# A two-layer graph kernel: two buffers for the divided weighted sums, their parts served after every product, and four changed places in the order

## The chip, the cores and the metric

The kernel runs on one core of a Trainium2 chip, all in fp32. A core has the engines TensorE (PE in the profile; PEld is its load of weights), VectorE (DVE), ScalarE (ACT) and GpSimd (POOL), and SyncE (SP), which here issues most of the DMAs. Each engine issues its instructions in the order in which the program has them; they wait for one another by semaphores. The metric is the time of one execution in microseconds of device time, smaller is better, as the median of several runs.

## The reference, cut to what matters

128 graphs of 64 nodes with 768 features go through two layers. `x` is (128, 64, 768), `adj` (128, 64, 64).

```python
# layer 0
u = h @ h.T / sqrt(d);  delta = softmax(u) * adjacency
attn = delta / (sum(delta) + 1e-10)
ctx = upper(attn) @ (h @ W_left.T + b_left) + diag(attn) * (h @ W_self.T + b_self) \
    + lower(attn) @ (h @ W_right.T + b_right)
x = layernorm(x + relu(normalise(ctx) * gamma + beta))
# layer 1, 12 heads of 64
q, k, v = heads(x @ Wq + bq), heads(x @ Wk + bk), heads(x @ Wv + bv)
s = where(adj > 0, q @ k.T / 8 + beta * adj, -9e15)
x = layernorm(x + softmax(s) @ v)
```

The part that the change is about is the last line: the product of the exponentials with `v`, its division by the row sums, and its addition to `x`.

## The kernel before, in words

The 8192 tokens are worked on in 16 blocks (`NBLK`) of 512 tokens: 8 graphs, held as 4 tiles of 128 rows. The loop over `n` (from L1205) interleaves three blocks: while block n does layer 1, block m = n+1 does layer 0, and block p = n-1 is finished (scores and weighted sums of its second group of heads, normalisation, store). In one turn of the loop TensorE does the left and right products of layer 0 for m, its self product, then values, queries and keys of layer 1 for n.

**Products.** All big products are done by schemes with fewer multiplications than the plain product, which need sums of inputs (POOL) and sums of outputs (DVE, some on ACT). The self product goes by `by_tokens` (matmuls L520, evictions L551 and L727). Left and right go by `side_part` (L756) for m below `DEEP` = 3, and for the 13 blocks from m = 3 by `both_sides` and `nested`: 49 sub-products of 7 groups of 7. Their matmuls are L784, their weights (`wlr`) come by DMA (L775). Each sub-product accumulates in one of two kinds of PSUM banks, X or Y. X takes the sub-products 1, 6, 7 and 4 of a group one after the other, Y takes 2, then 5 and 3, and DVE (L574) or ACT (L572) reads a bank between two of them: a late eviction holds up the next product of that bank. POOL adds the parts of the outer scheme (L581 to L589) and the inputs of the next group (`second_level`, the four sums of `q`, L472 to L475). Values, queries and keys go by `products`, a scheme of fifteen (matmuls L459, evictions L945 for `v`, L972 and L975 for queries and keys).

**The second half of the attention.** `scores(n, m)` does the scores of a group of heads (L996), their maximum and subtraction on DVE (L1008, L1012), the exponentials on ACT (L1029, 16 instructions of 0.52 us) into `eT`, and two transposes of `eT` on DVE, `turn` (L1033), of 0.97 us each. The two head groups use `eT` one after the other. `weighted(n, m)` does the weighted sums: 96 small matmuls (L1059) into four PSUM banks `ps_y`. Then come four parts `added(h, r)`: DVE takes the reciprocal of the row sums (L1065) and multiplies into a tile `share` (L1067), and POOL adds `share` to the rows of `x` in two adds (L1070). `share` has one buffer, so the next part's L1067 waits for both adds of the part before. `finish` follows: squares on ACT (L1116), mean and variance (L1089, L1092), root (L1095), reciprocal and shift (L1098, L1099), normalisation (L1103), store by POOL's queue (L1107).

**What sets the order.** There is no scheduler: instructions stand on each engine in the order in which the Python code issues them. Small work is not issued at once but put on one of three queues, `first`, `urgent` and `lazy`, and after each product (in `nested`: sub-product) `step` takes at most some items off them (`of_queues`, from L156). An item may have a kind ("act", "root", "tiny", "free", "gap"...); the four parts `added` have none and stand in `first`. In `nested` the steps after the sub-products 5, 1 and 3 are light: they leave `lazy` alone and run no item without a kind. `at(hooks, place, f)` puts a call at a place: `left` and `right` have 28 places together over the 49 sub-products (14 each), `val` and `qk` 15 each, one for each product. `freed` empties `first`, and `weighted` and `scores` call it. Layer 0's context (`context0`, matmuls L832, evictions L840) is put at four places of `val`.

Of the kernel before, what the change touches and what calls it, by code (L numbers as in the profile page):

```python
# [11 lines left out]
F32 = mybir.dt.float32  # L12
# [5 lines left out]
P = 128  # L18
B, L, D = 128, 64, 768
H, HD = 12, 64  # L20
# [14 lines left out]
THIRDS = 3  # L35
# [17 lines left out]
DEEP = 3  # L53
# [16 lines left out]
def gnn_two_layers(ctx: ExitStack, tc, x, adj, wl, bl, ws, bs, wr, br, gamma, beta,  # L70
# [12 lines left out]
    l0t = ctx.enter_context(tc.tile_pool(name="l0t", bufs=2))  # L83
# [54 lines left out]
    first, urgent, lazy = deque(), deque(), deque()  # L138

    def later(key, *fs, queue=lazy):  # L140
        queue.extend((key, f) if callable(f) else (key, *f) for f in fs)
# [18 lines left out]
    def of_queues(act_free, light):  # L160
        idle = not light
        for queue in (first, urgent) if light else (first, urgent, lazy):
            while queue and queue[0][2:] == ("free",):
                queue.popleft()[1]()
            if not queue:
                continue
            kind = queue[0][2] if len(queue[0]) > 2 else None
            if kind is None and not idle or kind in ("act", "root", "after") and not act_free:
                continue
            if kind == "after" and first:  # L170
                continue
            if kind == "root" and any(item[2:] == ("act",) for item in urgent):
                continue
            queue.popleft()[1]()
            idle = idle and kind is not None

    def freed():

        while first:
            first.popleft()[1]()  # L180
# [6 lines left out]
    def settle(key):  # L187

        for queue in (first, urgent, lazy):
            while any(item[0] == key or item[0][0] == key for item in queue):  # L190
                queue.popleft()[1]()
# [850 lines left out]
    def weighted(n, m):  # L1042


        blk = blocks[n]
        settle(("v", n))
        settle(("e", n, m))
        freed()
        xt, eT = blk["x"], blk["eT", m]
        by_parity = v.rearrange("p t (j g) d -> p t j g d", g=2)  # L1050
        y = {(h, r): ps_mm.tile([P, 2, THIRDS, HD + 1], F32, tag="mm", name=f"ps_y{r}") for h in range(2) for r in range(2)}
        for h in range(2):
            for t in range(2):
                for c in range(THIRDS):
                    for r in range(2):
                        rows = slice(r * L, (r + 1) * L)
                        for g in range(2):
                            cols = slice(g * L, (g + 1) * L)
                            nc.tensor.matmul(y[h, r][cols, t, c, :], lhsT=eT[rows, 2 * h + t, c, cols],  # L1059
                                             rhs=by_parity[rows, 2 * h + t, 2 * c + m, g, :], start=True, stop=True)  # L1060

        def added(h, r):
            ps = y[h, r]
            rz = st.tile([P, 2, THIRDS], F32, tag="rz1", name="rz1")
            nc.vector.reciprocal(rz, ps[:, :, :, HD])  # L1065
            share = l1_p.tile([P, 2, THIRDS, HD], F32, tag="share", name="share")
            nc.vector.tensor_tensor(share, ps[:, :, :, 0:HD], rz[:, :, :, None].to_broadcast([P, 2, THIRDS, HD]), ALU.mult)  # L1067
            for t in range(2):
                res = xt[2 * h + t].rearrange("p (c m r d) -> p m r c d", m=2, r=2, d=HD)[:, m, r]
                nc.gpsimd.tensor_tensor(res, res, share[:, t], ALU.add)  # L1070

        later(("y", n, m), *[partial(added, h, r) for h in range(2) for r in range(2)], queue=first)
# [116 lines left out]
    l1_p = ctx.enter_context(tc.tile_pool(name="l1", bufs=1))  # L1189
# [12 lines left out]
    for n in range(NBLK):  # L1202
        m, p = n + 1, n - 1
        left, right, own, val = {}, {}, {}, {}
        qk = [{}, {}]  # L1205

        def at(hooks, place, f, *args):
            hooks.setdefault(place, []).append(partial(f, *args))
# [13 lines left out]
        last = n == NBLK - 1  # L1222
        if p >= 0:
            one = left if not last else qk[0]
            at(one, 1, scores, p, 1, *((1,) if last else (2, None, 4)))
            at(one, 4 if last else 5 if m < DEEP else 6, weighted, p, 0)
            if not last:
                at(left, 13, weighted, p, 1)
                at(right, 4, finish, p)
            else:  # L1230
                at(qk[1], 3, weighted, p, 1)

        if not last:
            if n > 0:
                if m + 1 < NBLK:
                    at(left, 4, edges, m + 1)
                at(*((left, 11) if m < DEEP else (right, 13)), sides, m)
                sq1 = {}

                def begin1():  # L1240
                    blocks[n]["sq1"], sq1["fs"] = squares(blocks[n]["x_d"], nc.sync)


                when, place = right, 5 if m >= DEEP else 10
                at(when, place, begin1)
                fetch = {}

                def begin2():
                    fetch["fs"] = loads(m)

                at(val, 3, begin2)
                for t in range(T):
                    at(val, 3 + t, lambda t=t: fetch["fs"][t]())
                for a in range(P // Q):
                    at(when, place + a, lambda a=a: sq1["fs"][a]())
                at(own, 0, settle, ("f", p))

                def turn1():
                    blocks[n]["xT"] = turned(("t1", n), blocks[n]["sq1"], f"xT_{n}")
                    later(("m", n), *mask(n), queue=urgent)  # L1260

                at(own, 3, turn1)

                def sums1():
                    settle(("t1", n))
                    blocks[n]["S"] = fifteen(blocks[n]["xT"], False)

                at(own, 11, sums1)
                at(val, 0, lambda: fifteenth(blocks[n]["S"]))
                at(left, 6, lambda: combined4(blocks[m]["S"]))  # L1270
                if n > 1:
                    for k in range(T):
                        at(left, 1 + k, begun, ("o", n), T - 1 - k)
                at(*((left, 6) if n > 1 else (right, 1)), blocks[n]["stored"])
                if m + 1 < NBLK:
                    sq = {}

                    def begin():
                        blocks[m + 1]["sq"], sq["fs"] = squares(x_b[m + 1])

                    at(own, 11, begin)
                    for a in range(P // Q):
                        at(own if a < 3 else val, 11 + a if a < 3 else 0, lambda a=a: sq["fs"][a]())
                if m == DEEP:
                    settle("d")
                if m < DEEP:
                    side_part(m, "l", None, left)
                    side_part(m, "r", None, right)
                    at(own, 0, lambda: nc.vector.tensor_tensor(bias_lr[:, :, HALF:D], bias_lr[:, :, HALF:D],
                                                               bias_lr[:, :, 0:HALF], ALU.subtract))  # L1290
                else:
                    for t, f in enumerate(both_sides(m, {**left, **{2 * len(ORDER) + k: f for k, f in right.items()}})):
                        at(own, 1 + t, f)
                self_part(m, None, own)
            tiles, normal = context0(m)
            for place, f in zip((2, 3, 6, 7), tiles):
                at(val, place, f)
            for hooks, place, f in ((val, 10, normal[0]), (val, 14, normal[1]), (qk[0], 1, normal[2])):
                at(hooks, place, f)
            if m + 1 < NBLK:  # L1300

                def turn0():
                    blocks[m + 1]["hT"] = turned(("t", m + 1), blocks[m + 1]["sq"], f"hT_{m + 1}")

                at(val, 7, turn0)

                def scores0():
                    settle(("t", m + 1))
                    attention0(m + 1, False)

                def sums0():
                    blocks[m + 1]["S"] = combined(blocks[m + 1]["hT"], m + 1)

                at(qk[0], 3, scores0)
                at(qk[1], 10, sums0)
# [12 lines left out]
    n = NBLK - 1  # L1328
# [57 lines left out]
    def norm_by_act(t):  # L1386
        nc.scalar.activation(xt[t], xt[t], AF.Identity, bias=shift[:, t], scale=rstd[:, t])
        nc.sync.dma_start(out=out_t[n, t], in_=xt[t])

    values(n, {0: [partial(finish, n - 1, queue=lazy)], 1: [partial(scores, n, 1, 2, l0t)],  # L1390
               11: [partial(behind, (1, 2), (0, 0))], 13: [freed], 14: [partial(behind, (0, 1), (1, 0))]}, True)
    settle(("f", n - 1))
    divided, added = sixth(1, 1, ps_st)
# [62 lines left out]
```

## Time and profile before

| | |
|---|---|
| median of three runs | 2909.57 us (2909.15 to 2910.03) |
| the profiled execution's own time | 2913.13 us |
| its span (first to last instruction) | 2911.2 us |
| mean granted TensorE clock | 0.988 |
| POOL: share of the span, adds L1070 | 33%, 240 adds of 0.59 us |
| DVE: shares L1067 | 120 of 0.56 us |

The profile is taken from one execution; 1.93 us of its time lie outside the span, and it took 3.56 us longer than the median of the runs. Busy time is the time in which an engine executes; `PEclk` is the clock that TensorE was granted (1.00 is full). A row of the timeline gives start, duration, engine, line, operation, output and inputs, and in brackets how long the engine was idle before it and what it then waited for. A row of waits gives the sum in us, the number of times and the longest.

### The profile page before, as it was taken

Reading aid. Unit: us, or ns where it says so; the run is one execution under the profiler, and the core shown is the slowest. Engines: PE = TensorE matmul, PEld = TensorE weight load, DVE = VectorE, ACT = ScalarE, POOL = GpSimd, SP = SyncE. Lnnn points to the kernel's source line nnn. Section 1 sums busy time; section 2 is a strip of 40 time slices with the busy share of each in tenths; the row PEclk is TensorE's granted clock in tenths of the full one; section 3 lists DMA queues with packets and bytes.
Section 4 is the critical chain, followed back from the end, with each engine's and each line's share of the span. In section 5 each row is a group of like instructions: output and inputs, shape, how many; then the busy total and the mean of one; then the engine's idle time right before and its main releaser. Section 6 shows DMA issues by size and latency. Waiting matters only on the chain.

```text
span 2911.2 us, 49312 instructions
## 1 busy us (share of the span) xinstructions
PE 2810.4 (97%) x17962; PEld 2028.3 (70%) x17962; DVE 1949.7 (67%) x3399; ACT 1102.5 (38%) x1907; POOL 948.5 (33%) x1231
## 2 busy tenths in 40 slices
PE   8989999999999999999999999999999999999996
PEld 5557668586775857668586685867758577685885
DVE  5677767576675766757666675766757667576655
ACT  0002414335343452434425343343434524344254
POOL 3224232505135151431505225151351514315131
PEclk9999999999999999999999999999999999999998
DMA  8687595857759487684866758577584866848542
GB/s 312 214 283 256 162 311 160 255 156 238 210 180 260 124 276 189 199 245 148 260 173 208 235 162 256 152 243 206 187 245 131 272 187 199 243 139 262 163 119 90
DMA packets 398493, 604.85 MB, mean 208 GB/s; under 512 B 49296, under 2 KB 282256, under 8 KB 398256
## 3 DMA queue, kind: packets, MB, share of 16 engines
q1 hardware_dynamic: 349520, 506.73, 58.8%
q0 software_dynamic: 17456, 72.96, 6.6%
q10 hardware_dynamic: 31280, 22.03, 3.7%
q8 instruction: 145, 2.38, 0.3%
q14 instruction: 92, 0.75, 0.1%
HBM read 530.00 MB, written 78.45 MB: 209 GB/s over the span
## 4 chain that ended last, share of the span: by engine, by line
PE 86%; DVE 5%; POOL 4%; DMA 3%; issue 1%; ACT 1%; SPq 1%; DVEq 0%; ACTq 0%
PE ps_X L459 25%; PE ps_Y L459 17%; PE ps_X L520 11%; PE ps_Y L784 9%; PE ps_X L784 8%; PE ps_Y L520 8%; PE ps_ctx L832 3%; POOL o L1070 2%; PE u L663 2%; PE ps_y L1059 2%; PE sc L996 2%; DVE share L1067 1%; DMA wlr<-lr_d 1%; DVE u_deep L574 1%; DVE lr L574 1%
## 5 line engine op out<-in xcount | busy, mean ns | idle before, releaser
L408 POOL TENSOR_TENSOR sums<-hT 128x768 f32<-128x768 f32 x16 | 28.9, 1808 | 852.2 <-PE ps_X L459 840.6
L1029 ACT ACTIVATE eT<-s 32x384 f32<-32x384 f32 x512 | 266.6, 521 | 31.7 <-DVE s L1012 25.4
L843 ACT ACTIVATE unused<-o 128x768 f32<-128x768 f32 x60 | 50.6, 843 | 497.1 <-DVE o L840 211.6
L459 PE MATMUL ps_X<-xT,wqk 128*128 128x256 f32 x1024 | 234.3, 379 | 3.4 <-DMA wqk<-qk_d 2.6
L574 DVE TENSOR_TENSOR lr<-ps_Y,u_deep 128x384 f32<-128x384 f32 x273 | 151.9, 557 | 102.5 <-PE ps_Y L784 83.8
L459 PEld LDWEIGHTS ps_X<-xT,wqk 128*128 128x128 f32 x1024 | 194.3, 190 | 30.8 <-DVE w_deep L362 3.0
L784 PE MATMUL ps_Y<-wlr,q 128*128 128x384 f32 x546 | 208.6, 491 | 0.0
L972 ACT ACTIVATE qk<-ps_X,bq 128x256 f32<-128x256 f32 x128 | 60.7, 474 | 387.4 <-PE ps_X L459 387.1
L975 DVE TENSOR_TENSOR qk<-qk,ps_X 128x512 f32<-128x512 f32 x160 | 109.8, 686 | 136.3 <-PE ps_X L459 72.2
L784 PE MATMUL ps_X<-wlr,q 128*128 128x384 f32 x364 | 153.0, 503 | 38.7 <-POOL o L1070 38.7
L520 PE MATMUL ps_X<-ws,hT 128*128 128x384 f32 x540 | 181.4, 490 | 3.0 <-DVE u L551 3.0
L459 PE MATMUL ps_Y<-more,wqk 128*128 128x256 f32 x768 | 181.4, 379 | 0.0
L459 PE MATMUL ps_X<-sums,wqk 128*128 128x256 f32 x768 | 180.3, 381 | 0.5 <-issue 0.5
L1070 POOL TENSOR_TENSOR o<-o,share 128x192 f32<-128x192 f32 x240 | 136.7, 591 | 111.7 <-DVE share L1067 92.0
L459 PEld LDWEIGHTS ps_Y<-more,wqk 128*128 128x128 f32 x768 | 145.9, 190 | 19.8
L459 PEld LDWEIGHTS ps_X<-sums,wqk 128*128 128x128 f32 x768 | 144.6, 190 | 20.9 <-issue 0.9
L520 PEld LDWEIGHTS ps_X<-ws,hT 128*128 128x128 f32 x540 | 103.0, 191 | 75.7 <-DVE u L551 4.0
L975 DVE TENSOR_TENSOR qk<-qk,ps_Y 128x512 f32<-128x512 f32 x160 | 108.2, 677 | 65.2 <-PE ps_Y L459 62.6
L784 PEld LDWEIGHTS ps_Y<-wlr,q 128*128 128x128 f32 x546 | 101.6, 190 | 67.2
L574 DVE TENSOR_TENSOR u_deep<-ps_X,lr 128x384 f32<-128x384 f32 x195 | 107.7, 552 | 55.8 <-PE ps_X L784 49.5
L784 PEld LDWEIGHTS ps_X<-wlr,q 128*128 128x128 f32 x364 | 67.8, 192 | 95.3 <-POOL o L1070 41.7
L437 POOL TENSOR_TENSOR more<-xT 128x512 f32<-128x512 f32 x32 | 43.1, 1348 | 276.8 <-DVE xT L396 182.1
(269 smaller groups left out, 6296.8 us busy)
## 6 DMA issues: line engine op xcount, KB each, us to landing
wlr<-lr_d SPq DMA_DIRECT2D x819, 192.0 KB, 4.1
wqk<-qk_d SPq DMA_DIRECT2D x480, 256.0 KB, 2.6
wv<-v_d SPq DMA_DIRECT2D x240, 256.0 KB, 6.1
ws<-d_s SPq DMA_DIRECT2D x180, 192.0 KB, 4.8
ws<-in_L_gnn_W_self_dram SPq DMA_DIRECT2D x135, 192.0 KB, 6.0
xa<-in_x_dram SPq DMA_DIRECT2D x64, 384.0 KB, 5.6
out_dram<-o POOLq DMA_DIRECT2D x60, 384.0 KB, 6.6
sq<-in_x_dram ACTq DMA_DIRECT2D x56, 384.0 KB, 10.9
```

What stands on the lines that cost most here:

```text
L459: nc.tensor.matmul(ps[:, h, :], lhsT=a, rhs=b, start=start and h == 0 and k == 0, stop=k == len(fs[h]) - 1, skip_group_check=True)
L520: nc.tensor.matmul(ps, lhsT=a, rhs=b, start=(c == 0 and i in (1, 2, 5)), stop=(c == len(fs) - 1), skip_group_check=True)
L574: nc.vector.tensor_tensor(dst, view(ps), add, ALU.add)
L663: nc.tensor.matmul(u[g * L : (g + 1) * L, t, :], lhsT=xT[:, c, tok], rhs=xT[:, c, tok], start=(c == 0), stop=(c == KC - 1))
L784: nc.tensor.matmul(ps, lhsT=a, rhs=b, start=(k == 0 and j in (1, 2, 5)), stop=(k == len(fs) - 1), skip_group_check=True)
L832: nc.tensor.matmul(ps[g * L : (g + 1) * L, 0:HALF], lhsT=blk["aT"][:, t, g * L : (g + 1) * L], rhs=blk["lr"][t][:, g, h * HALF : (h + 1) * ...
L972: nc.scalar.activation(dst[:, h], ps[:, h, :], AF.Identity, bias=bias["qk"[h]][:, c : c + 1], scale=float(sign))
L975: nc.vector.tensor_tensor(dst, dst, ps, ALU.add if sign > 0 else ALU.subtract)
L996: nc.tensor.matmul(sc[t // 2, r][g * L : (g + 1) * L, t % 2, c, :], lhsT=q[rows, c, tok], rhs=k[rows, c, tok], start=True, stop=True)
L1029: nc.scalar.activation(e[to[0], :, to[1]], pairs[rows, :, cols], AF.Exp, scale=1.0 / SCALE)
L1059: nc.tensor.matmul(y[h, r][cols, t, c, :], lhsT=eT[rows, 2 * h + t, c, cols], rhs=by_parity[rows, 2 * h + t, 2 * c + m, g, :], start=True, ...
L1070: nc.gpsimd.tensor_tensor(res, res, share[:, t], ALU.add)
```

## The change

It does six things.

1. In a light step, an item of `first` without a kind (a part `added`) is run too (L168).
2. `share` has two buffers (L1066).
3. The weighted sums of the first group start at place 5 of `left` in all blocks, not at 6 from m = 3 on (L1226). For 13 blocks this is one group of sub-products sooner.
4. For m below 3, the weighted sums of the second group start at place 1 of `right` instead of 13 of `left`, and `finish` at place 6 of `right` instead of 4 (L1228). Only n = 1 has such a block p.
5. In the first turn (n = 0) all four tiles of the context are put at place 0 of `val`, not at 2, 3, 6 and 7 (L1296).
6. In the last values, the scores of the second group have seven gaps instead of one ahead of their transposes (L1390), so that both transposes are issued later.

```diff
 of_queues
-            if kind is None and not idle or kind in ("act", "root", "after") and not act_free:
+            if kind is None and not idle and not (light and queue is first) or kind in ("act", "root", "after") and not act_free:
 weighted, added
-            share = l1_p.tile([P, 2, THIRDS, HD], F32, tag="share", name="share")
+            share = l1_p.tile([P, 2, THIRDS, HD], F32, tag="share", name="share", bufs=2)
 the loop over n
-            at(one, 4 if last else 5 if m < DEEP else 6, weighted, p, 0)
+            at(one, 4 if last else 5, weighted, p, 0)
             if not last:
-                at(left, 13, weighted, p, 1)
-                at(right, 4, finish, p)
+                at(*((left, 13) if m >= DEEP else (right, 1)), weighted, p, 1)
+                at(right, 4 if m >= DEEP else 6, finish, p)
...
-            for place, f in zip((2, 3, 6, 7), tiles):
+            for place, f in zip((2, 3, 6, 7) if n > 0 else (0, 0, 0, 0), tiles):
                 at(val, place, f)
 after the loop
-    values(n, {0: [partial(finish, n - 1, queue=lazy)], 1: [partial(scores, n, 1, 2, l0t)],
+    values(n, {0: [partial(finish, n - 1, queue=lazy)], 1: [partial(scores, n, 1, 2, l0t, 7)],
```

## The prediction

> **What bounds the kernel now.** I read the page first, then the waits of PE, then the timeline of one block (840 to 905 us), then the windows by clock.
>
> ```profile
> span 2911.2 us, 49312 instructions
> PE 2810.4 (97%) x17962; PEld 2028.3 (70%) x17962; DVE 1949.7 (67%) x3399; ACT 1102.5 (38%) x1907; POOL 948.5 (33%) x1231
> PE 86%; DVE 5%; POOL 4%; DMA 3%; issue 1%; ACT 1%; SPq 1%; DVEq 0%; ACTq 0%
> ```
>
> TensorE sets the time: 97% busy, 86% of the chain. This change removes no matmul, so all it can win is PE's idle time and time at a lower clock. The waits of PE say where that is (total, times, longest), and those of DVE what is behind it:
>
> ```profile
> PE ps_X L784 <- POOL o L1070: 38.7, 26, 2.6
> PE ps_y L1059 <- DVE eT L1033: 4.1, 2, 2.9
> PE ps_X L784 <- DMA wlr<-lr_d: 2.4, 4, 0.9
> ```
> ```profile
> DVE share L1067 <- POOL o L1070: 58.9, 36, 2.9
> ```
>
> The first is the largest wait: 26 times, two in each of the 13 blocks with nested left and right products. The timeline shows the long one:
>
> ```profile
> 879.39 1.00 POOL L581 TENSOR_TENSOR lr<-lr 128x384 f32<-128x384 f32 x1
> 879.54 0.56 DVE L1067 TENSOR_TENSOR share<-ps_y,rz 128x384 f32<-128x384 f32 x1
> ...
> 881.41 1.00 POOL L589 TENSOR_TENSOR lr<-lr,lr 128x384 f32<-128x384 f32 x1
> 881.58 0.51 PEld L784 LDWEIGHTS ps_Y<-wlr,sums 128*128 128x128 f32 x2
> ...
> 882.37 1.13 POOL L1070 TENSOR_TENSOR o<-o,share 128x192 f32<-128x192 f32 x2
> ...
> 883.53 0.56 DVE L1067 TENSOR_TENSOR share<-ps_y,rz 128x384 f32<-128x384 f32 x1 [2.87 <-POOL o L1070]
> ...
> 884.66 0.56 DVE L574 TENSOR_TENSOR u_deep<-ps_X,lr 128x384 f32<-128x384 f32 x1
> ...
> 885.32 0.88 PE L784 MATMUL ps_X<-wlr,q 128*128 128x384 f32 x2 [2.61 <-POOL o L1070]
> ```
>
> The share of 879.54 waits for its two POOL adds, which stand behind three sums of POOL (879.39 to 882.4). The next share needs the same buffer, so it waits until 883.53, and DVE issues in order: the two L574 evictions behind it are late, and PE's next product needs the last one's bank. The short wait (0.36 us at 866.26) has the same shape.
>
> **What the two waits cost.** Where PE is dense, pairs of weight loads start 0.645 us apart. Long wait: from 881.58 the load after next was due at 882.87 and came at 885.72, so 2.85 us are lost; by the same count the short wait loses 0.60, and the second group's weighted sums lose 0.26 (1.82 us instead of 1.56) to their transposes. That is 3.71 us a block. Then the clock (columns: stretch, its length, busy time of PE, PEld, DVE, ACT, POOL, then PEclk):
>
> ```profile
> 708.60:712.00 3.40, 3.40 (x6) 1.77 (x7) 1.67 (x3) 1.26 (x4) 3.32 (x6) 0.56 0.98 195
> 1414.00:1417.40 3.40, 3.33 (x11) 2.04 (x12) 2.06 (x5) 1.41 (x4) 3.32 (x7) 1.00 1.14 197
> ```
>
> After the long wait PEclk is 0.55 to 0.66 in ten of 13 blocks (first row) and 1.00 in three (second row: eleven matmuls instead of six). The low stretches are 3.41 us long and cost 1.7 us: at 886.37 six loads take 3.62 us instead of 1.94, and the block period is 176.8 us with one, 175.1 without. So ten blocks lose 5.40 us, three 3.71.
>
> [...]
>
> **Part 1: two share buffers, and the divided sums run after every product.** The orders of both programs, side by side, show that the four recip-and-share pairs (0.22 + 0.48 us) now follow each other closely, so that POOL gets the adds before L581, L588 and L589. I replayed the block with the durations of the timeline: share and reciprocal 0.70, an L574 eviction 0.56 (0.65 if the next depends on it), a pair of adds 1.13, the four q sums (L472 to L475) 2.04, a transpose L1033 0.89.
>
> First weighted sums, one sub-group earlier (853.75 instead of 855.28): share 1 at 857.61, share 2 at 858.79 without a wait, adds 1 at 858.26 to 859.39, share 3 at 859.49. POOL then has the q sums (to 861.40) ahead of adds 2 (to 862.53), so share 4 waits until 862.60: the old wait returns one share later, but the product behind it starts 0.2 us late at most. Next in DVE's new order is the second group's first transpose L1033, which used to come several products later and now stands ahead of an lr and a u_deep eviction. It needs the exps. Their table load followed the weighted sums by 0.2 us (857.42); now it can start at 855.48, so 1.28 + 8.52 us of ACT end at 865.29. The transpose runs from 865.32 to 866.21, u_deep is out at 867.41, and PE, due at 865.41, starts at 867.48: some **1.85 us lost**, a wait in the place of the 0.60. PE would stand idle for some 1.6 us. PE's idle waits of 1.64 (370.5) and 1.86 (222.8) are followed by no low clock in this trace, one of 1.91 (2784.7) is, so I price none; the margin is thin.
>
> Second weighted sums: the transposes are done (0.26 regained) and share 4 behind the q sums costs 0.24. A block then loses 2.09 instead of 5.40 or 3.71: 10 x 3.31 + 3 x 1.62 = **38.0 us**. The x1d stores and L420 come later on POOL; the store's readers start some 15 us later, so I cost that at nothing.
>
> What it triggers: PE comes 2 to 3 us earlier to a stretch in which the DMA engines are full (share 0.96 to 1.15 after the wait). The bounds are nothing and all 38 us. The nearest rows are the three blocks that had no low clock and so came 1.7 us sooner: together they lost one wlr wait of 0.66, 0.2 us each. A step twice as long should lose more than in proportion; I take 0.6 a block, **8 us** off.
>
> **Part 2: n=1.** Weighted sums of the second group wait twice, then the clock falls (340.38, 3.41 us):
>
> ```profile
> 338.36 0.93 PE L1059 MATMUL ps_y<-v,eT 64*64 64x65 f32 x48 [2.90 <-DVE eT L1033]
> 340.51 1.58 PE L1059 MATMUL ps_y<-v,eT 64*64 64x65 f32 x48 [1.22 <-DVE eT L1033]
> ```
>
> 2.90 + 1.22 + 1.7 = 5.8 us. Twelve matmuls of 0.322 (3.9 us) now go ahead, which covers nearly all. But 30 us on PE waits for wr loads (0.62 + 1.64), and those don't come sooner, so up to 2.3 is given back: 2 to 6, I take **4**.
>
> **Part 3: n=0.** PE waits 5.34 us, from 211.9 to 217.25, for POOL's sums. One group of 16 context matmuls moves from behind this wait ahead of it, 2.80 us, and its four L840 fall into DVE's idle 6.71 us before 213.53. The wait's end is set by POOL, so **2.7** is saved; 0 if DVE's L840 delay the first v evictions, 4.4 if the low clock at 214.09 shrinks by half.
>
> **Part 4: the end.**
>
> ```profile
> 2872.49 1.84 DVE L1033 STREAM_TRANSPOSE eT<-eT 128x768 f32<-128x768 f32 x2 [6.47 <-ACT eT L1029]
> ...
> 2875.83 1.48 PE L459 MATMUL ps_Y<-wv,more 128*128 128x256 f32 x4 [4.49 <-DVE v L945]
> ```
>
> The transposes leave the place ahead of the v evictions, but L1098 is left there, and it waits for ACT's root (2873.97), which stands behind the same exps and a table load. L1098 takes the transposes' place; evictions follow from 2874.3 and PE starts at 2875.0: **0.8** (0 to 1).
>
> **Sum.** 38.0 + 4 + 2.7 + 0.8 - 8 = 37.5. The profiled execution took 2913.13 us (its span, and 1.93 around it), so 2875.6; it lay 3.56 above the median of the runs, so 2872.1 against 2909.57. A measurement of this kernel can tell about 0.2% (5.8 us) from no change.
>
> **Rivals.**
> - Forecast, 0.48: 2872, by itself 2860 to 2881.
> - The clock falls after the new wait, 0.17. If the wait at the transpose is some 0.3 us longer than replayed, ten blocks keep their low stretch: 17 us less, 2889. For it: my margin is 0.3 us. Against: a wait counts only where it falls well on the grid of 3.41.
> - The transposes don't block, 0.15. If the exps are done in time, 13 x 1.85 = 24 more is saved: 2848. For it: the exps start sooner. Against: their 8.52 us.
> - The wlr loads set the pace after 877, 0.09. Then the 38 go, and 7.5 are left: 2902, at the edge of what can be told (0.02 for the same). For it: DMA share above 1. Against: median slack of a wlr load is 5 to 8 us.
> - Slower, 0.11 (0.03 the same, 0.08 slower). One mechanism, at the transpose L1033 ahead of the evictions: if the exps start no sooner than now, its wait grows by 1.94 and the low clock follows in all 13 blocks: 1.85 + 1.94 + 1.7 + 0.24 = 5.73, level with now. From there each further us costs 13: one more table load (1.28) gives 10 x 1.61 + 3 x 3.30 - 7.5 = 18.5 more than now, 2928.
>
> Faster 0.87, same 0.05, slower 0.08. The first three cases hold 0.80; with the bounds of the small parts they reach from 2846 to 2893.
>
> **What would show it.** The L1067 wait on L1070 drops from 58.9 us, and PE's L784 wait on L1070 (38.7) all but goes; a PE wait for u_deep L574 of 1.5 to 2 us appears 13 times, with L1033 waiting for ACT in the same place; PEclk is 1.00 after 886; ps_y waits for eT vanish. No wait at L1033, or wlr waits far above 8 us, would prove me wrong.

## The result and the profile after

The changed kernel is slower by a little: 2919.33 us (median of 20 runs, 2908.24 to 2935.97) against 2910.2 (20 runs, 2903.94 to 2916.92), a ratio of 1.0031 with a 95% interval of 1.002 to 1.0043. The forecast was 2872.1. The profiled execution took 2916.36 us, with a span of 2914.3. The parts of the page that answer to those of before:

```profile
span 2914.3 us, 49295 instructions
PE 2807.8 (96%) x17962; PEld 2019.9 (69%) x17962; DVE 1950.4 (67%) x3399; ACT 1101.7 (38%) x1907; POOL 945.0 (32%) x1231
PE 85%; DMA 7%; DVE 4%; issue 2%; POOL 1%; SPq 1%; ACT 1%; DVEq 0%; POOLq 0%; ACTq 0%
```

In the chain that ended last POOL fell from 4% to 1%, and DMA rose from 3% to 7%. The waits of PE and of DVE after (sum, times, longest) say the same with lines:

```profile
PE ps_X L784 <- DMA wlr<-lr_d: 36.6, 14, 5.3
PE ps_X L784 <- issue: 17.6, 12, 1.5
...
PE ps_X L784 <- POOL o L1070: 1.8, 1, 1.8
```
```profile
DVE share L1067 <- POOL o L1070: 34.8, 29, 1.3
```

The wait for the adds (38.7 us before) is gone but for one of 1.8 us, and a wait for the weights `wlr` of nearly the same sum (2.4 before) stands in its place. The row "issue" is a new wait, which the timeline resolves as one at the transpose L1033; the 1.8 us of the last row fall at the same place of another block:

```profile
857.57 0.98 DVE L1033 STREAM_TRANSPOSE eT<-eT 128x768 f32<-128x768 f32 x1 [0.64 <-ACT eT L1029]
858.47 0.52 DVE L574 TENSOR_TENSOR lr<-ps_Y,u_deep 128x384 f32<-128x384 f32 x1
...
859.09 0.56 DVE L574 TENSOR_TENSOR u_deep<-ps_X,lr 128x384 f32<-128x384 f32 x1
...
859.75 0.89 PE L784 MATMUL ps_X<-wlr,q 128*128 128x384 f32 x2 [1.46 <-issue]
```

The transpose waits for ACT's exponentials, the evictions of `lr` and `u_deep` stand behind it on DVE, and PE starts 0.1 us after the second has ended.

**Where the time went, by stretches of both traces.** From the start to the first nested matmul: 480.2 us after, 490.7 before, 10.5 less. From there to the last nested matmul: 2197.2 against 2181.6, 15.6 more. From there to the last matmul of the program: 219.1 against 221.1. The gain of the small moves was real; the 13 nested blocks lost more than that. In them PE's gaps went from 45.2 to 61.3 us, while the time at the low clock fell from 34.1 us to 27.3 (the granted clock is 0.5 there, so half of it is lost).

**The load that is late.** SP's rows and PE's rows of the same block after:

```profile
693.70 2.24 SPq L775 DMA_DIRECT2D wlr<-lr_d  x5
696.17 1.39 SPq L387 DMA_DIRECT2D sq<-x1d  x3
697.61 10.63 SPq L775 DMA_DIRECT2D wlr<-lr_d  x9
```
```profile
702.64 0.81 PE L784 MATMUL ps_X<-wlr,q 128*128 128x384 f32 x2
707.80 1.62 PE L784 MATMUL ps_X<-wlr,sums 128*128 128x384 f32 x2 [4.36 <-DMA wlr<-lr_d]
```

At 693.70 a weight buffer comes free, and SP issues five `wlr` loads, three `sq<-x1d` loads (which read block n back for layer 1) and the nine `wlr` loads of the last group. By the trace's semaphores the three `sq` loads landed at 703.34, 705.27 and 707.38, two us apart, and the first `wlr` load behind them at 707.66. So 14 us pass from the free buffer to the landed load, and PE asked for it after 9.7. Before:

```profile
704.00 2.69 SPq L775 DMA_DIRECT2D wlr<-lr_d  x5
706.91 1.38 SPq L387 DMA_DIRECT2D sq<-x1d  x3
708.34 0.56 SPq L775 DMA_DIRECT2D wlr<-lr_d  x1
```
```profile
708.52 1.14 PE L784 MATMUL ps_X<-wlr,q 128*128 128x384 f32 x2 [2.62 <-POOL o L1070]
...
718.02 0.81 PE L784 MATMUL ps_X<-wlr,sums 128*128 128x384 f32 x2
```

The same order with the same spacing, and the load landed at 717.30. PE came to it at 718.02, 14.0 us after the buffer came free, because the old wait of 2.62 us and 1.7 us of low clock lay in between. It was in time by 0.7 us. The removed wait had been hiding the loads' order.

The trace before holds nearly the whole sum. In the 13 blocks this load landed 0 to 4.0 us before it would have held PE up, 20.8 us together. By the prediction's own figures the change takes 2.85 us out of PE's way to it in each block and 1.7 us of low clock in ten, 54.1 us together. So 54.1 - 20.8 = 33.3 us should come back as waits for this load. In these 13 places PE waits 35.8 us after, and no block differs from its own sum by more than 1.6 us.

### The profile page after: what moved, and what is told of

It reads as the page before. It is cut to its first block, busy times and chain, and to the rows that moved or that the text cites. A ratio compares the mean times of both kernels' runs of the same rounds, so it can differ in the third digit from the quotient of the medians.

```text
span 2914.3 us, 49295 instructions
## 1 busy us (share of the span) xinstructions
PE 2807.8 (96%) x17962; PEld 2019.9 (69%) x17962; DVE 1950.4 (67%) x3399; ACT 1101.7 (38%) x1907; POOL 945.0 (32%) x1231
## 4 chain that ended last, share of the span: by engine, by line
PE 85%; DMA 7%; DVE 4%; issue 2%; POOL 1%; SPq 1%; ACT 1%; DVEq 0%; POOLq 0%; ACTq 0%
PE ps_X L459 25%; PE ps_Y L459 17%; PE ps_X L520 10%; PE ps_Y L784 10%; PE ps_X L784 8%; PE ps_Y L520 7%; DMA wlr<-lr_d 4%; PE ps_ctx L832 3%; PE sc L996 2%; PE u L663 2%; PE ps_y L1059 2%; DMA h_q<-in_L_gnn_Wq_dram 0%; POOL o L1070 0%; ACT eT L1029 0%; DMA h_v<-in_L_gnn_Wv_dram 0%
## 5 line engine op out<-in xcount | busy, mean ns | idle before, releaser
L574 DVE TENSOR_TENSOR u_deep<-ps_X,lr 128x384 f32<-128x384 f32 x195 | 107.7, 553 | 66.7 <-PE ps_X L784 61.3
L784 PE MATMUL ps_X<-wlr,sums 128*128 128x384 f32 x234 | 93.7, 510 | 38.6 <-DMA wlr<-lr_d 35.8
```

Of the source, the lines that this page charges most:

```text
L574: nc.vector.tensor_tensor(dst, view(ps), add, ALU.add)
L784: nc.tensor.matmul(ps, lhsT=a, rhs=b, start=(k == 0 and j in (1, 2, 5)), stop=(k == len(fs) - 1), skip_group_check=True)
```

## The experiments

Theory A is what was just read: an order of loads on SP's queue. Theory B says that the stretch simply holds too many bytes. Theory C says that the new wait at the transposes is the loss, and the `wlr` wait its result. Ratios are to the kernel before on the same chip, where its medians were 2911.7 to 2912.2 us.

**All four `sq` loads behind the last `wlr` loads, in the changed kernel.**

```diff
-                when, place = right, 5 if m >= DEEP else 10
+                when, place = right, 8 if m >= DEEP else 10
```

> The changed kernel, with the four sq<-x1d loads of the 13 nested blocks begun at place 8 of right, not 5, so that all stand behind the last nine wlr loads on SP's queue instead of three ahead of them. Theory A (a load order): after the change PE reaches the last group but one before its wlr load has landed, because that load stands behind three sq loads of 384 KB; in the profile after, it is issued 3.9 us after SP had a free buffer and lands 8.4 to 10.9 us later. Then PE's wait for wlr (36.6 us) falls below 6, six low-clock stretches in the blocks go, and the time is 2919 - 33 - 12 = 2874, say 2868 to 2885. Theory B (transfers: the stretch has too many bytes in whatever order): the wait moves to ws loads or to the transposes of sq, and the time is 2910 to 2920. Theory C (the new wait of 1.47 us at the transpose L1033 is the loss, the wlr wait only a result of it): 2915 to 2922.

Measured: 2917.27 us, 1.0015 (1.0002 to 1.0028). Theory A's time was missed by 43 us; the time lies in the ranges of B and of C, and the wait for `ws` that B named is there, so this run speaks against neither. The `wlr` waits did go, but three others stand in PE's list:

```profile
PE ps_X L784 <- POOL q L473: 16.7, 13, 1.3
PE ps_X L520 <- DMA ws<-in_L_gnn_W_self_dram: 14.8, 12, 6.0
PE ps_X L784 <- issue: 10.5, 8, 1.5
PE ps_X L784 <- POOL o L1070: 8.8, 6, 1.5
```

The last two rows together are the wait at the transposes (the trace puts it to one or the other), which was there before the edit too. New are the `ws` loads, which now stand behind the four `sq` loads, and POOL's sums `q` for the last group. My reading was that the loads' order matters, but that this order only moves the late load, and a POOL wait of 1.3 us a block had been hidden as well.

**The same edit in the kernel before.**

> The kernel before with that one edit alone. Theory A: there PE came late to the same load because of the share wait, so the load cost next to nothing (wlr waits 2.4 us): 2906 to 2911. Theory B: the same or slower, 2910 to 2920. Theory C says nothing of it.

Measured: 2968.73 us, 1.0188 (1.0171 to 1.0206). Both theories were wrong in the size, though B had the direction. The page of waits has the share wait unchanged and a new one:

```profile
PE ps_X L784 <- POOL o L1070: 38.7, 26, 2.6
PE ps_X L520 <- DMA ws<-in_L_gnn_W_self_dram: 37.3, 20, 6.3
```

I had not thought of what stands behind the last `wlr` loads: `ws`, which PE needs at once. The low-clock time in the nested stretch also rose, from 34 to 65 us (mean granted clock 0.984, before 0.988). Which load is late depends on what is put ahead of it. Why the `ws` loads cost 40 us here and 18 in the changed kernel, no run shows.

**The three small moves alone** (points 4, 5 and 6 of the change, on the kernel before).

```diff
+                at(*((left, 13) if m >= DEEP else (right, 1)), weighted, p, 1)
+                at(right, 4 if m >= DEEP else 6, finish, p)
...
+            for place, f in zip((2, 3, 6, 7) if n > 0 else (0, 0, 0, 0), tiles):
...
+    values(n, {0: [partial(finish, n - 1, queue=lazy)], 1: [partial(scores, n, 1, 2, l0t, 7)],
```

> The kernel before with the three small moves alone (second weighted sums of n=1, context tiles of n=0, seven gaps at the end). The traces have the first nested matmul at 490.7 us before and 480.2 after, and 3.69 instead of 4.49 us of wait at the end: all theories 10.5 + 0.8 less, 2896 to 2902. If the nested blocks pass it on to another wait, it is less.

Measured: 2897.69 us, 0.9953 (0.9939 to 0.9968), 14.5 us less. They are worth what the traces said, and a little more.

**Later transposes in the changed kernel.**

```diff
-            at(one, 1, scores, p, 1, *((1,) if last else (2, None, 4)))
+            at(one, 1, scores, p, 1, *((1,) if last else (2, None, 8)))
```

> The changed kernel with eight gaps instead of four ahead of the second group's transposes L1033, so that these come three evictions later. Theory A: the wait of 1.47 us goes, and PE waits that much longer for the wlr load: 2914 to 2920. Theory C: 13 x 1.47 = 19 us less and more by the clock, 2890 to 2900.

Measured: 2905.43 us, 0.9974 (0.9962 to 0.9985), 14 below the changed kernel's median, or 17 by the two ratios. The wait at the transposes is gone, and the `wlr` wait is as it was:

```profile
PE ps_X L784 <- DMA wlr<-lr_d: 37.0, 14, 5.1
```

The time lies between the ranges of A and C. The wait at the transposes lies 10 us and more before the buffer comes free at which SP's loads start. It shifts PE and the loads alike, so the late load does not hide it: of its 19 us, 14 to 17 were won. Only a wait between a load's issue and its use is hidden by the load. So theory C had a part of the loss (14 to 17 where it said 19), and A the other.

**The `sq` loads spread.** The changed kernel with eight gaps, and one `sq` load ahead of the last but one nine `wlr` loads, one ahead of the last nine, two ahead of `ws`; then two, one and one.

```diff
-                at(when, place, begin1)
+                places = (3, 5, 8, 10) if m >= DEEP else (10, 11, 12, 13)
+                at(when, places[0], begin1)
...
-                    at(when, place + a, lambda a=a: sq1["fs"][a]())
+                    at(when, places[a], lambda a=a: sq1["fs"][a]())
```

> The changed kernel with eight gaps ahead of the transposes, and the four sq<-x1d loads spread on SP's queue: one ahead of the last but one nine wlr loads, one ahead of the last nine, two ahead of the ws loads. Theory A (order: three loads in a row in front of nine small ones make those late): neither wlr nor ws waits, below 6 us in sum; left is the POOL wait of 1.3 us a block that the kernel with all four behind showed (q L473), so 2917 - 19 - 18 - 7 (low clock after ws waits) = 2873, say 2866 to 2882. Theory B (too many bytes in the stretch, whatever their order): waits on DMA of 30 us stay, 2900 to 2915.

Measured: 2873.07 us, 0.9868 (0.9854 to 0.9883). Theory A's number was 2873. That it fits to the microsecond is luck: the sum kept 16.7 us of waits for POOL's `q`, of which 7.7 came, and counted 7 us for a low stretch of 6.8 us, which costs half of that.

```profile
PE ps_X L784 <- POOL q L473: 7.7, 10, 1.3
PE ps_X L784 <- DMA wlr<-lr_d: 6.8, 11, 1.0
```

The same bytes in the same stretch, and 30 us of waits for weights are gone, and with them all low clock in the nested blocks (mean granted clock 0.995, before 0.988). Theory B, which had 30 us of waits on DMA stay, falls.

> The same, two sq loads ahead of the last but one nine wlr loads, one ahead of the last nine, one ahead of ws. Theory A: as the spread before, 2866 to 2885, some us more if SP has to wait for the stores of x1d. Theory B: 2900 to 2915.

(Places 1, 3, 5 and 8.) Measured: 2889.58 us, 0.9925 (0.9905 to 0.9945). Between the theories: with two `sq` loads together, `wlr` waits of 28.4 us come back, in 19 places of at most 2.8:

```profile
PE ps_X L784 <- DMA wlr<-lr_d: 28.4, 19, 2.8
```

**Parts of the change alone, on the kernel before.** First two buffers and light steps (both lines), then the buffers alone (the second).

```diff
+            if kind is None and not idle and not (light and queue is first) or kind in ("act", "root", "after") and not act_free:
...
+            share = l1_p.tile([P, 2, THIRDS, HD], F32, tag="share", name="share", bufs=2)
```

> The kernel before with two share buffers and the light steps alone, the weighted sums in their old places. Theory A: the share waits go and PE waits for the same wlr load instead: L1070 waits fall from 38.7 us below 5, wlr waits rise to 25 to 40; against before within 10 us, 2905 to 2922. If the earlier first weighted sums did the harm, it is below 2895.

Measured: 2970.29 us, 1.0201 (1.0182 to 1.0221), far outside. The `wlr` waits are as expected, but another is larger:

```profile
PE ps_X L784 <- issue: 46.6, 13, 3.8
PE ps_X L784 <- DMA wlr<-lr_d: 35.2, 14, 6.1
```

3.56 us in nearly every block, with a low clock behind it. At the same spot the transpose L1033 waits 2.69 us for the exponentials. Light steps empty `first` sooner, so `urgent` moves up and issues the transposes before ACT is done; with the weighted sums at their old place the exponentials start later, and the wait is 3.56 instead of 1.47. Low-clock time in the nested stretch is 82 us (mean granted clock 0.979).

> The kernel before with two share buffers alone. The fourth share then waits only for the adds of the second, which are done: the long L1070 wait goes. Theory A: the wlr wait takes its place, 2905 to 2920. Theory C (nothing behind the wait): 13 x 2.85 + 10 x 1.7 = 54 less, 2858.

Measured: 2902.71 us, 0.9972 (0.9959 to 0.9985). As theory A has it, if 2 us below its range: the second buffer by itself takes away both share waits, and the `wlr` wait takes their place. The waits at the transposes are not there, so the `wlr` wait is not their result, as theory C had it.

```profile
PE ps_X L784 <- DMA wlr<-lr_d: 33.4, 14, 5.7
```

**The change without its light steps.**

```diff
-            if kind is None and not idle and not (light and queue is first) or kind in ("act", "root", "after") and not act_free:
+            if kind is None and not idle or kind in ("act", "root", "after") and not act_free:
```

> The changed kernel with the light steps as before (parts 2 to 6 alone). Theory A with the light steps as the harmful part (they bring the transposes L1033 ahead of evictions before the exps are done): the 1.47 us waits go, the wlr waits of 33 to 37 us stay. Two buffers alone gave 2903 and the three small moves 14.5, so 2888, say 2880 to 2900. If the earlier first weighted sums do harm by themselves, 2905 or more.

Measured: 2908.22 us, 0.999 (0.998 to 1.0). The light steps cost the change some 11 us, but the sum of the parts (9.3 and 14.5 less) would be 2888, so the earlier weighted sums cost some 20 by themselves, if the parts add up. PE's list shows most of it:

```profile
PE ps_X L784 <- DMA wlr<-lr_d: 34.8, 14, 4.8
PE ps_X L784 <- POOL o L1070: 14.2, 13, 1.1
```

At place 5 a share wait comes back (1.09 us a block). It lies before the loads' issue, so it is paid too.

**The change without light steps, with the loads spread as in the run of 2873 us, at place 5 and at place 6.** The second has, besides:

```diff
-            at(one, 4 if last else 5, weighted, p, 0)
+            at(one, 4 if last else 5 if m < DEEP else 6, weighted, p, 0)
```

> The same, with the four sq<-x1d loads spread one, one, two as in the run that gave 2873. Theory A: 30 us of wlr waits and 10 of low clock less than without the spread: 2845 to 2862. If POOL's sums q are late by then as in the run with all four behind (1.3 us a block): up to 2870.

Measured: 2878.47 us, 0.9892 (0.9873 to 0.991): 8 us above the range, whose upper end allowed for POOL's `q` wait (16.4 here) but not for the share wait just named, which stands at 14.2 us here too.

> As the last, but the first weighted sums at their old place 6 (parts 2, 4, 5, 6 and the spread). Within 8 us of the last, 2848 to 2870; this tells what the earlier place is worth without the light steps.

Measured: 2861.88 us, 0.983 (0.9808 to 0.9852). This is the fastest kernel of the study: two buffers, the small moves, spread loads, and nothing else of the change. It differs from the last only in the place, which is worth 16.6 us, twice what I had allowed for. What PE waits for now:

```profile
PE ps_X L784 <- POOL q L473: 17.5, 13, 1.6
...
PE ps_X L784 <- DMA wlr<-lr_d: 1.8, 3, 1.0
```

**The spread alone, on the kernel before** (the diff of the spread, places 3, 5, 8 and 10).

> The kernel before with the spread alone. Theory A: there the share wait is the one that ends last, the wlr load was in time, so nothing is won: L1070 waits stay at 38 us, 2903 to 2912. If the loads' order cost time on its own account (clock, transposes of sq), 2870 to 2895.

Measured: 2912.02 us, 0.9998 (0.9988 to 1.0008). Nothing, as theory A needs: the share wait (38.8 us) ends last there. The loads' order costs nothing until that wait is gone, and then it costs most of what the removal would give (the buffers alone won 9 us).

## Why the prediction was wrong, point by point

- **What bounds the kernel, and what the two waits cost:** right. The waits fell to 1.8 us, and two buffers alone do that.
- **First weighted sums and the wait at the transpose:** right. Replayed idle 1.6 us, measured 1.47 in nearly every block, and no low clock after it. Setting it against the loss of 0.60 was right too: both lie ahead of the issue of the late loads, so neither is hidden by them (14 to 17 us in the run with later transposes).
- **What it triggers, "0.6 a block, 8 us off": here it failed.** Measured: 36.6 us of `wlr` waits and six low stretches with 27 us in the nested blocks, half of it lost: some 50 us where 8 stood, of which the trace before gives 33 by the sum above. I took three blocks that had lost little, and of a load's slack the median, 5 to 8 us over all `wlr` loads. The number that mattered was in the same trace: the first `wlr` load behind three `sq` loads lands 7.7 to 10.6 us after its issue, and in five of the 13 blocks PE came to it less than 0.8 us after its landing. The old wait lay between that load's issue and its use, so its removal could win no more than the slack of the block, 20.8 us in all.
- **The rival "the wlr loads set the pace" (0.09, 2902)** was the mechanism. Its price was 17 us too low, since it let the new wait of 1.47 us be hidden with the rest: 13 x (1.47 - 0.36) = 14.
- **Parts 2, 3 and 4:** 2.7 and 4 us forecast for n=0 and n=1, 10.5 measured to the first nested matmul. At n=0 PE's wait fell from 5.34 to 2.47 us. At n=1 the waits for the transposes (2.90 and 1.22) went but for 0.23 us, and the wait for `wr` shrank to 0.99 instead of growing. The end gave 0.80 (4.49 to 3.69), as worked out.
- **Order of the other rivals:** the low clock did not follow the new wait; the "slower" rival named the transposes, and they do slow the kernel by that mechanism, most of all with the weighted sums at their old place (2970).

## What to carry to other kernels

Before a wait is priced as a gain, list the loads that are issued before it and used after it: for these it is cover, and in each block the gain ends at the smallest of their slacks there, not at a median. A wait that lies before the issue covers nothing, and its removal is won (here 14 to 17 us of 19). When a wait is gone and the time is not, look for the next in the list, here a load behind three larger ones on one queue, and change the order before the sizes.

## What the runs showed of the hardware

- Loads issued on SP's queue landed in the order of issue in this stretch: three of 384 KB two us apart, then `wlr` loads of 192 KB half a us apart, with the DMA engines full (share 1.06 to 1.10). How long a load took to land went with what was issued ahead of it: a `wlr` load took 2.2 us at the least, and 8.4 to 10.9 behind three `sq` loads (profile after).
- Whether the clock fell went with where a wait lay. In each of the two profiles, before and after, all low stretches of the nested blocks (ten and six) begin on one grid of 3.413 us, to within 5 ns, and last one or two steps of it at a granted clock of 0.5. Two waits of the profile after:

```profile
1237.70 1.08 PE L784 MATMUL ps_X<-wlr,sums 128*128 128x384 f32 x2 [2.59 <-DMA wlr<-lr_d]
1950.12 0.88 PE L784 MATMUL ps_X<-wlr,sums 128*128 128x384 f32 x2 [3.64 <-DMA wlr<-lr_d]
```

The wait of 2.59 us (from 1235.11) lies whole in one step of the grid, and a low stretch begins at its end, 1238.25. The longer one (from 1946.48) straddles the grid line at 1948.22, with 1.74 us on one side and 1.90 on the other, and no low stretch follows. The next two rows are a stretch that begins within the wait of 4.36 us and one that begins within a wait of 1.80 (PEclk is the third last column):

```profile
705.70:709.10 3.40, 1.30 (x2) 0.84 (x3) 0.00 (x0) 0.00 (x0) 3.24 (x5) 0.51 1.06 342
884.50:887.90 3.40, 2.09 (x7) 1.32 (x8) 1.86 (x4) 1.13 (x2) 3.24 (x5) 1.00 1.06 358
```

The idle time in each step can be counted. The nested blocks of the two profiles hold 1263 steps of the grid at full clock. The 16 that a low stretch followed held 2.03 us or more without a matmul; of the 1247 others, none held more than 1.90. Outside the nested blocks the least ahead of a low stretch was 1.91 us (from 2784.32, before), so the two kinds lie close. Still, in these two profiles the idle time within one step of 3.413 us tells the two kinds apart, and the length of a wait by itself does not (2.59 us was followed by a low stretch, 3.64 was not). The ends of matmuls are modelled in these records, and the figures carry the error of that.
